# A four-layer graph network on one core: the last layer's messages, products and norm steps in another order

## The chip, the core and the metric

One core of a Trainium2 chip runs the whole program: sixteen independent graphs, one after the other, in 32-bit floats throughout. The engines are named as the profile names them: PE (TensorE, matrix products), PEld (its weight loads), DVE (VectorE), ACT (ScalarE), POOL (GpSimd) and SP (SyncE, which here issues nearly all DMAs). The metric is device microseconds of one execution; lower is better. Before the change three runs took 2419.71, 2419.86 and 2420.47 us, a median of 2419.86 us.

## The reference

For each of 16 graphs there are 1024 nodes with 128 features (`x`) and a 1024 by 1024 weighted adjacency (`adj`). Two networks run in a row, each followed by a residual and a layer norm:

```
# first network
degree = adj.sum(-1)
s      = einsum('bid,bij->bjd', x, adj) / degree
x      = layernorm(x + relu(concat(x, s) @ W.T + b))
# second network: four layers on f (at first f = x)
src_agg = einsum('bjv,bij->biv', f @ ws + bs, adj / l2norm(adj, axis 2))
dst_agg = einsum('bjv,bji->biv', f @ wd + bd, adj / l2norm(adj, axis 1))
f       = tanh(concat(src_agg, f @ wn + bn, dst_agg) @ wu + bu)
# layer three reads f of layers two and one; layer four f of three and two, and x
x       = layernorm(x + f)
```

## The kernel before, in words

**Products.** `wu` is folded into the three other weights ahead of everything, so a layer is: messages (features times folded weights, a DST and a SRC half), then an aggregate (messages times the scaled adjacency and its scaled transpose, added up in PSUM). Each aggregate is a Strassen-Winograd scheme: seven products M1, M2, M3, M4, Z11, Z12, Z21 of half-size operands in place of eight. Its operand sums are made on DVE: `T[2]`, `T[3]`, `T[4]` from the adjacency `a` (for DST), `Q[2..4]` from the transpose `at` (for SRC), and `S[2..4]` from the messages `X` (`message_sums`). The result of M1 to M4 is put together from PSUM by ACT copies and DVE additions into `e0` and `e12`.

**Two columns of PE.** Each product uses 64 of PE's 128 columns, and `aggregate` writes out two lists, `upper` and `lower`, that run side by side. `in_turn` interleaves them. The numbers in `events` and `hooks` are positions in `upper`: at that position the named function's instructions are issued to their engines, ahead of the product of that position.

**Order of work.** The program is scheduled by hand: each engine executes its instructions in the order in which the Python code emits them, and waits on semaphores where data or buffers demand it. In one turn of the loop over `b` the second network of graph `b` runs, with the first network of graph `n = b + 1` and the norm of graph `b - 1` slipped in: layer one (`aggregate` with `l` 0), layer two (`l` 1), layer three's messages (`paired_messages` with `l` 2) and aggregate, then the first network of graph `n` (`first_gnn`), then layer four's messages (`l` 3) and aggregate. Fifteen turns prepare a next graph; the sixteenth doesn't.

**Where the norm of the next graph sits.** Its steps are functions handed to layer four: `add0`, `spread0`, `sum0`, `centre0`, `squares0` by the dictionary `between`, called at the places `at(0)` to `at(4)` of `paired_messages`, and `rstd0`, `rows0`, `end0`, `quarters0`, `rows1`, `rows2` by `hooks` of its aggregate. `centre0` holds a small PE product (`pm`), and an ACT square; `squares0` a DVE reduction to `v`; `rstd0` a small PE product of `v` (`pv`), the DVE sum `ve`, and a power on POOL (line 456); `end0` the DVE multiplication by it (line 461), and `quarters0` the next graph's `T[2]` and `T[3]` (lines 678 and 680).

**Column norms of the next graph.** In layer two of graph `b` the column sums of squares of graph `n` are reduced to `part` (line 344). `inverses` multiplies them on PE (`pc`), takes them to DVE and raises them on POOL (line 376); `inverse_rows`, called by `factors`, finishes them on DVE, writes them to DRAM (`dr`, line 402), and `factor_row` reads them back as a row on all partitions (`cinv`, line 408). The sixteen multiplications of line 414 scale the next adjacency by it.

**Banks.** PSUM has eight banks here: two for Z0 and Z1, four that rotate under the tag `pt` (message products, and `Bk`, `A`, `Dk`, `Ck` for M2, M1, M3, M4), and two that rotate under the tag `small`. M3's SRC part is accumulated in `A` once M1 has been copied out of it.

Of the kernel before, what the change touches and what calls it, by code (L numbers as in the profile page):

```python
# [15 lines left out]
NL = 4  # L16
CHUNKS = [1, 1, 2, 3]
G = 4
# [5 lines left out]
def adj_resnorm_kernel(ctx: ExitStack, tc: tile.TileContext, x, adj, w0, b0, layers, out):  # L24
# [33 lines left out]
    nc = tc.nc  # L58
# [12 lines left out]
    def blocks(ap):  # L71

        return ap.rearrange("p (k g c) -> p g k c", g=G, c=C)
# [627 lines left out]
                between[n]()  # L701
        return message_sums(b, l, t) if with_sums else t

    def message_sums(b, l, t, amid=lambda: None):
# [7 lines left out]
        amid()  # L712
        nc.vector.tensor_sub(S[2], S[1], X[0, 0])
        nc.vector.tensor_sub(S[4], X[0, 1], S[2])
        return X, S
# [9 lines left out]
    def paired_messages(b, l, w, wm, rest=None, between={}):  # L725

        t = [one.tile([P, NJ, 2, 2, V], F32, tag=f"t{j}", name=f"t{l + 1}_{b}_{j}") for j in range(2)]
        X = {(v, j): t[j][:, :, :, v] for v in range(2) for j in range(2)}
        y, s, T2, T4 = w["y"], message_seven(wm), w["T2"], w["T4"]
        T3 = w["e0"] = one.tile([P, HW], F32, tag="e0", name=f"e0_{l}_{b}")  # L730
        o = own_seven(l, wm)
        w["own"] = {"M1": (o["w00"], y[0, 0]), "M2": (o["S2"], T2), "M3": (o["S3"], T3), "M4": (o["S1"], y[0, 1]),
                    "Z11": (o["w01"], y[1, 0]), "Z12": (o["S4"], y[1, 1]), "Z21": (o["w11"], T4)}

        def bank(i):
            return product(f"pt{l + 1}_{b}_{i}")

        def parts(pt):
            return pt.rearrange("p (k a c) -> p k a c", k=NJ, a=2)

        def into(pt, *terms):
            for i, (f, x) in enumerate(terms):
                for k in range(NJ):
                    by_halves(pt[:, k * P:(k + 1) * P], f[:, k * P:(k + 1) * P], x, i == k == 0,
                              i == len(terms) - 1 and k == NJ - 1)
            return pt

        def plain(v, h):
            return [(rest[:, half(h)], wm[:, MREST + v * P:MREST + (v + 1) * P])] if rest is not None else []

        def bias(v):
            return wm[:, v * P:(v + 1) * P].rearrange("p (a c) -> p a c", a=2)[:, None].to_broadcast([P, NJ, 2, V])

        def add(to, x, pt):
            nc.vector.tensor_add(X[to], X[x], parts(pt))  # L755

        def add_sbuf(to, x):
            nc.vector.tensor_add(X[to], X[to], X[x])  # L758

        def add_bias(to, x, v):  # L760
# [12 lines left out]
        if l == 2:  # L773
            m4 = into(bank(4), (y[0, 1], s["S1"]))
            nc.scalar.copy(X[1, 1], parts(m4))
            m1 = into(bank(1), (y[0, 0], s["w00"]))
            add_bias((0, 0), parts(m1), 0)
            at(0)
            t3()
            t4()  # L780
            z12 = into(bank("z12"), (y[1, 1], s["S4"]))
            m2 = into(bank(2), (T2, s["S2"]))
            add((0, 1), (0, 0), m2)
            m3 = into(bank(3), (T3, s["S3"]))
            add((1, 0), (0, 1), m3)
            at(1)
            add_sbuf((0, 1), (1, 1))
            add((0, 1), (0, 1), z12)
            z11 = into(bank("z11"), (y[1, 0], s["w01"]))
            add((0, 0), (0, 0), z11)  # L790
            z21 = into(small(f"pt{l + 1}_{b}_z21", [HW]), (T4, s["w11"]))
            at(2)
            add_bias((1, 0), X[1, 0], 1)
            add_sbuf((1, 1), (1, 0))
            add((1, 0), (1, 0), z21)
        else:
            t4()
            t3()
            m4 = into(bank(4), (y[0, 1], s["S1"]))
            nc.scalar.copy(X[1, 1], parts(m4))  # L800
            at(0)
            m1 = into(bank(1), (y[0, 0], s["w00"]))
            add_bias((0, 0), parts(m1), 0)
            at(1)
            z11 = into(bank("z11"), (y[1, 0], s["w01"]), *plain(0, 0))
            at(2)
            z12 = into(bank("z12"), (y[1, 1], s["S4"]), *plain(0, 1))
            m2 = into(bank(2), (T2, s["S2"]))
            add((0, 1), (0, 0), m2)
            add((0, 0), (0, 0), z11)  # L810
            at(3)
            m3 = into(bank(3), (T3, s["S3"]))
            add((1, 0), (0, 1), m3)
            add_bias((1, 0), X[1, 0], 1)
            add_sbuf((0, 1), (1, 1))
            add((0, 1), (0, 1), z12)
            add_sbuf((1, 1), (1, 0))
            z21 = into(small(f"pt{l + 1}_{b}_z21", [HW]), (T4, s["w11"]), *plain(1, 0))
            add((1, 0), (1, 0), z21)
            p11 = into(bank("p11"), *plain(1, 1))  # L820
            add((1, 1), (1, 1), p11)
        XS = message_sums(b, l, t, lambda: at(4))
        if l == 2:
            at(3)
        return XS

# [27 lines left out]
    def aggregate(b, l, feats, msgs, wm, a, at, T, Q, fT, etag, hooks={}, pieces=1, w=None):  # L854
# [9 lines left out]
        else:  # L864
            e0, e12 = w["e0"], w["e12"]
            Bk, A, Dk, Ck = (product(f"m{i}_{l}_{b}") for i in (2, 1, 3, 4))
        e1, e2 = e12[:, 0], e12[:, 1]
        Z0, Z1 = (product(f"z{h}_{l}_{b}", h) for h in range(NH))

# [22 lines left out]
            nc.scalar.copy(e1[low], e0[high])  # L892

        def m3_read():
            nc.vector.tensor_add(e0[high], e0[high], A[high])
            nc.scalar.copy(e1[high], e0[high])

        def second_half():
# [54 lines left out]
        else:  # L953
            rest = [(f, c) for f, c in feats if c not in PAIRED[l]]

            own_of = {name: [(x, blocks(f))] for name, (x, f) in w["own"].items()}
            m3, m3s = prod("M3", DST), prod("M3", SRC)
            shared = [[(*m3[-1], slice(i * HW // 2, (i + 1) * HW // 2))] for i in range(2)]
# [23 lines left out]
            else:  # L982
                upper = [
                    (Z1, True, own(1, 1, rest)), (Z0, True, own(1, 0, rest)), *own_upper,
                    (A, False, m1), (Bk, False, m2[:NJ]), (A, True, m3s[:1] + shared[1]),
                    (Bk, False, m2[NJ:]), (A, False, m3s[1:]),
                    (Z0, False, prod("Z21", SRC) + prod("Z21", DST)),
                ]
                lower = [
                    (Z1, True, own(0, 1, rest)), (Z0, True, own(0, 0, rest)), *own_lower,  # L990
                    (Dk, False, m3[:2]), (Ck, True, m4[:NJ]), (Dk, False, m3[2:-1]), (Ck, False, m4[NJ:]),
                    (Z1, False, z12[:1]), (Dk, False, shared[0]), (Z1, False, z12[1:]), (Z0, False, prod("Z11", SRC) + prod("Z11", DST)),
                ]
                events = {13: m1_read, 17: m4_read, 19: m3_half, 23: m2_and_half_of_m3, 26: last_reads}

        for i, (o, x, y_, start, stop) in in_turn(flat_steps(upper, high), flat_steps(lower, low)):
            if i in events:
# [235 lines left out]
    for b in range(B):  # L1233
# [162 lines left out]
            p.update(begin_paired(b, 2, f1, f2, "acc"))  # L1396

        hooks = alongside(hooks, {11: y4, 27: t2})
        if b == 0:
            hooks = alongside(hooks, {12: lambda: weight_sums(own_seven(3, None))})  # L1400
        aggregate(b, 1, feats, t, wm, a, at, T, Q, f23, "row", hooks)
        wm = ahead["wm"]
        if b:
            second_norm, xs2 = w, w.get("xs")
            if nxt:
                inverses(n, st)


        feats = [(f1, 1), (f23, 0)]
# [72 lines left out]
        if nxt:  # L1482
# [35 lines left out]
            def place(i, a=a):  # L1518
                return a[:, 2 * i:2 * i + 2].rearrange("p k (u c) -> p (k u) c", c=NH * P)

            def rows0():
                for i, q in enumerate((2, 3)):
                    rows[q] = load_rows(n, q, [place(i)])
                half_of_rows(1, 1, "sq", two)

            def end0(w=w):
                norm_end(w["ys"], w["r"], KS)
                w["x1"] = one.tile([P, N], F32, tag="xb", name=f"x1_{n}_T")
                for h in range(NH):
                    x1_features(n, w["ys"], h, w["x1"])  # L1530
                w["kept"] = put_aside(n, w["ys"])

            def quarters0(w=w):
                half_of_rows(0, 1, "acc")
                w["T"] = combined(n, "T")
                for i in (2, 3):
                    combine(i, y2, w["T"])
                scale_rows(rows[2], 2, rinv)

            def rows1(w=w):  # L1540
# [7 lines left out]
                scale_rows(rows[1], 1, rinv)  # L1548

            between = {0: add0, 1: spread0, 2: sum0, 3: centre0, 4: squares0}  # L1550
            hooks = {7: rstd0, 11: rows0, 14: end0, 18: quarters0, 23: rows1, 27: rows2}
        else:
            x1v = one.tile([P, N], F32, tag="x", name="x1_last")
            for h in range(NH):
# [83 lines left out]
```

## Time and profile before

| what | us |
|---|---|
| median of three runs | 2419.86 |
| the profiled execution's own time | 2422.51 |
| its span, first to last instruction | 2420.7 |
| PE busy | 2391.8 (99%) |
| DVE busy | 2086.4 (86%) |
| ACT busy | 973.3 (40%) |
| POOL busy | 274.4 (11%) |
| POOL power of 128x32, mean of 30 | 6.387 |
| DVE step over 128x512, line 414, mean of 250 | 0.692 |
| matrix product of 512 columns, mean | 0.592 to 0.594 |

A row of the timeline reads: start, length, engine, line, operation, out<-in, shape, count, and in brackets the idle time ahead of it with what ended it. Products overlap in the records: one of 512 columns is shown as 0.59 us long, but in an unbroken stretch one pair, upper and lower, follows the other every 0.429 us, and a 32-bit product is two such passes. A position of `upper` is therefore 0.858 us. A PE that is shown as busy can still be late; the starts have to be compared.

### The profile page before, as it was taken

To read this page: it belongs to the slowest core of one execution; us is meant where nothing else is said; L and a number is where in the kernel's file an instruction comes from. 1 tells how busy PE (TensorE), PEld (TensorE's weight loads), DVE (VectorE), ACT (ScalarE), POOL (GpSimd) and SP (SyncE) were. 2 spreads that over 40 slices of the span, in tenths; PEclk is the share of its full clock that TensorE was granted. 3 is DMA by queue.
4 is the path that set the end of the run, shared out by engine and by line. 5 is a ranking of instruction groups with operands and counts; after the bars stand their busy time and mean duration, and the time that the engine had idled before them with its cause. 6 is when DMAs were issued, how large, how long until landed. Compare 5 with 4: busy or idle time off the path is not lost. (4 is left out here: it accounts for less than half of the span.)

```text
span 2420.7 us, 38913 instructions
## 1 busy us (share of the span) xinstructions
PE 2391.8 (99%) x15293; PEld 1083.8 (45%) x15293; DVE 2086.4 (86%) x2799; ACT 973.3 (40%) x1827; POOL 274.4 (11%) x102
## 2 busy tenths in 40 slices
PE   8999999999999999999999999999999999999998
PEld 4454444444444445444444445444444444444544
DVE  5988989989898998889988899898998989899864
ACT  5524345253342634426244362434525334263322
POOL 4101111011111011110111100111101111101100
PEclk9999999999999999999999999999999999999999
DMA  8627344272533726335282452724427253372400
GB/s 186 139 66 153 69 103 87 71 157 56 127 73 77 149 48 145 71 80 130 48 166 50 97 113 62 154 67 101 90 71 157 57 124 77 78 148 48 99 21 22
DMA packets 365895, 232.01 MB, mean 96 GB/s; under 512 B 152784, under 2 KB 336848, under 8 KB 365712
## 3 DMA queue, kind: packets, MB, share of 16 engines
q1 hardware_dynamic: 364944, 227.16, 43.4%
q0 software_dynamic: 768, 2.36, 0.4%
q8 instruction: 121, 1.98, 0.4%
q14 instruction: 62, 0.51, 0.1%
HBM read 209.59 MB, written 19.84 MB: 95 GB/s over the span
## 5 line engine op out<-in xcount | busy, mean ns | idle before, releaser
L1001 PE MATMUL m<-Q,S 128*64 128x512 f32 x1008 | 450.7, 593 | 0.0
L1001 PE MATMUL m<-at,t 128*64 128x512 f32 x1008 | 439.3, 594 | 0.0
L1001 PE MATMUL m<-T,S 128*64 128x512 f32 (+1 forms) x1072 | 439.2, 567 | 0.0
L1001 PE MATMUL m<-a,t 128*64 128x512 f32 x1008 | 425.1, 593 | 0.0
L456 POOL TENSOR_TENSOR rs<-ve,mhalf 128x32 f32<-128x32 f32 x30 | 191.6, 6387 | 1938.0 <-DVE ve L454 1938.0
L1001 PEld LDWEIGHTS m<-Q,S 128*64 128x64 f32 x1008 | 135.6, 137 | 266.9 <-issue 248.5
L883 ACT COPY e<-m 64x512 f32<-64x512 f32 x63 | 36.6, 582 | 516.1 <-PE m L1001 515.7
L1001 PE MATMUL z<-at,S 128*64 128x512 f32 x504 | 229.2, 592 | 0.0
L1001 PE MATMUL z<-at,t 128*64 128x512 f32 x504 | 229.2, 592 | 0.0
L1001 PE MATMUL z<-a,S 128*64 128x512 f32 x504 | 227.0, 593 | 0.0
L1001 PE MATMUL z<-a,t 128*64 128x512 f32 x504 | 226.8, 592 | 0.0
L1001 PE MATMUL z<-Q,t 128*64 128x512 f32 x504 | 226.6, 592 | 0.1
L1001 PEld LDWEIGHTS m<-T,S 128*64 128x64 f32 x1072 | 134.7, 137 | 150.7 <-issue 137.4
L1001 PEld LDWEIGHTS m<-a,t 128*64 128x64 f32 x1008 | 127.3, 137 | 116.2 <-issue 109.1
L1001 PEld LDWEIGHTS m<-at,t 128*64 128x64 f32 x1008 | 129.2, 137 | 112.0 <-issue 99.4
L1001 PE MATMUL z<-T,t 128*64 128x512 f32 x384 | 172.8, 592 | 0.0
L414 DVE TENSOR_TENSOR a<-a,cinv 128x512 f32<-128x512 f32 x250 | 154.2, 692 | 15.0 <-DMA cinv<-dr 6.8
L322 ACT ACTIVATE sq<-a 128x1024 f32<-128x1024 f32 x120 | 126.0, 1051 | 66.7 <-DVE acc L331 63.3
L1001 PEld LDWEIGHTS z<-Q,t 128*64 128x64 f32 x504 | 69.0, 137 | 142.7 <-issue 141.1
L317 ACT ACTIVATE a<-a 128x1024 f32<-128x1024 f32 x120 | 124.9, 1042 | 0.0
L247 PE MATMUL pt<-wm,f1T 128*64 128x128 f32 (+1 forms) x1536 | 120.6, 310 | 0.0
L331 DVE TENSOR_TENSOR acc<-acc,sq 128x1024 f32<-128x1024 f32 x90 | 110.0, 1222 | 7.2 <-ACT sq L322 3.6
(295 smaller groups left out, 4725.1 us busy)
## 6 DMA issues: line engine op xcount, KB each, us to landing
a<-in_adj_dram SPq DMA_DIRECT2D x120, 512.0 KB, 13.3
rows<-in_adj_dram SPq DMA_DIRECT2D x480, 64.0 KB, 2.1
a<-in_adj_dram SPq DMA_DIRECT2D x240, 128.0 KB, 4.2
wm<-wsave SPq DMA_DIRECT2D x32, 704.0 KB, 5.3
wm<-wsave SPq DMA_DIRECT2D x31, 320.0 KB, 3.8
xn<-in_x_dram SPq DMA_DIRECT2D x124, 64.0 KB, 5.5
xs<-in_x_dram SPq DMA_DIRECT2D x60, 128.0 KB, 3.6
cinv<-dr SPq DMA_DIRECT2D x30, 256.0 KB, 6.4
```

The lines of the kernel that those rows point to most:

```text
L247: nc.tensor.matmul(out[s], x[:, s], y, start=start, stop=stop)
L317: nc.scalar.activation(a[:, i, :], a[:, i, :], AF.Copy, accum_out=degree)
L322: nc.scalar.activation(sq, a[:, i, :], AF.Square, accum_out=state["cols"][:, i:i + 1])
L331: nc.vector.tensor_add(state["acc"], state["acc"], state[i])
L414: engine.tensor_mul(a[:, i, s], a[:, i, s], cinv[:, s])
L456: nc.gpsimd.tensor_tensor(rstd, ve, mhalf[:, :n], ALU.pow)
L883: nc.scalar.copy(e0[high], A[high])
L1001: nc.tensor.matmul(o, x, y_, start=start, stop=stop)
```

## The change

Seven edits, six of them in layer four.

1. Layer four's message products come in the order M4, M1, M2, Z11, M3, Z12, Z21 (before: M4, M1, Z11, Z12, M2, M3, Z21), and the places `at(1)` to `at(4)` move with them. `at(4)` (`squares0`) now stands ahead of `message_sums` instead of in its middle.
2. In its aggregate the order is M1's first half of DST, M2's DST, M3's SRC, then M1's rest; below, M3's DST without a break, then M4.
3. M3's SRC part gets a bank `G` of its own from the tag `small`, in layer four alone. The reads (`events`) move.
4. The hooks: `rstd0` at 5 (before 7); `rows0` is split: the first quarter of rows and the next graph's `T[2]` at 11 (`quarter0`), the other rows at 15 with `end0` (before 14), which also makes the next `T[3]`. `quarters0` at 18 loses both.
5. Layer three: `at(1)` goes from behind M3's addition to ahead of Z12's and M2's products. For `b` of 1 and more that is `factors`; for `b` 0 nothing hangs there.
6. Layer two, for `b` of 1 to 14: `inverses` is issued at hook 29, one position ahead of the aggregate's end, and no longer behind it.
7. `message_sums` loses its argument `amid`.

```diff
         if l == 2:
...
             t4()
+            at(1)
             z12 = into(bank("z12"), (y[1, 1], s["S4"]))
             m2 = into(bank(2), (T2, s["S2"]))
             add((0, 1), (0, 0), m2)
             m3 = into(bank(3), (T3, s["S3"]))
             add((1, 0), (0, 1), m3)
-            at(1)
...
         else:
...
             at(1)
-            z11 = into(bank("z11"), (y[1, 0], s["w01"]), *plain(0, 0))
-            at(2)
-            z12 = into(bank("z12"), (y[1, 1], s["S4"]), *plain(0, 1))
             m2 = into(bank(2), (T2, s["S2"]))
             add((0, 1), (0, 0), m2)
-            add((0, 0), (0, 0), z11)
-            at(3)
+            at(2)
+            z11 = into(bank("z11"), (y[1, 0], s["w01"]), *plain(0, 0))
             m3 = into(bank(3), (T3, s["S3"]))
             add((1, 0), (0, 1), m3)
             add_bias((1, 0), X[1, 0], 1)
+            z12 = into(bank("z12"), (y[1, 1], s["S4"]), *plain(0, 1))
             add_sbuf((0, 1), (1, 1))
+            at(3)
+            add((0, 0), (0, 0), z11)
+            add_sbuf((1, 1), (1, 0))
             add((0, 1), (0, 1), z12)
-            add_sbuf((1, 1), (1, 0))
             z21 = into(small(f"pt{l + 1}_{b}_z21", [HW]), (T4, s["w11"]), *plain(1, 0))
             add((1, 0), (1, 0), z21)
             p11 = into(bank("p11"), *plain(1, 1))
             add((1, 1), (1, 1), p11)
-        XS = message_sums(b, l, t, lambda: at(4))
+            at(4)
+        XS = message_sums(b, l, t)
...
+            if l == NL - 1:
+                G = small(f"m3s_{l}_{b}", [HW])
...
-                    (A, False, m1), (Bk, False, m2[:NJ]), (A, True, m3s[:1] + shared[1]),
-                    (Bk, False, m2[NJ:]), (A, False, m3s[1:]),
+                    (A, False, m1[:2]), (Bk, False, m2[:NJ]), (G, True, m3s[:1] + shared[1]), (A, False, m1[2:]),
+                    (Bk, False, m2[NJ:]), (G, False, m3s[1:]),
...
-                    (Dk, False, m3[:2]), (Ck, True, m4[:NJ]), (Dk, False, m3[2:-1]), (Ck, False, m4[NJ:]),
-                    (Z1, False, z12[:1]), (Dk, False, shared[0]), (Z1, False, z12[1:]), ...
+                    (Dk, False, m3[:-1]), (Ck, True, m4[:NJ]), (Dk, False, shared[0]), (Ck, False, m4[NJ:]),
+                    (Z1, False, z12), ...
-                events = {13: m1_read, 17: m4_read, 19: m3_half, 23: m2_and_half_of_m3, 26: last_reads}
+                events = {14: m3_half, 18: m4_read, 19: m1_read, 23: m2_and_half_of_m3, 26: last_reads}
...
+        if b and nxt:
+            hooks = alongside(hooks, {29: lambda: inverses(n, st)})
...
-            if nxt:
-                inverses(n, st)
...
-            def rows0():
-                for i, q in enumerate((2, 3)):
-                    rows[q] = load_rows(n, q, [place(i)])
+            def quarter0(w=w):
+                w["T"] = combined(n, "T")
+                combine(2, y2, w["T"])
+                rows[2] = load_rows(n, 2, [place(0)])
+
+            def end0(w=w):
+                rows[3] = load_rows(n, 3, [place(1)])
                 half_of_rows(1, 1, "sq", two)
-
-            def end0(w=w):
                 norm_end(w["ys"], w["r"], KS)
                 w["x1"] = one.tile([P, N], F32, tag="xb", name=f"x1_{n}_T")
                 for h in range(NH):
                     x1_features(n, w["ys"], h, w["x1"])
                 w["kept"] = put_aside(n, w["ys"])
+                combine(3, y2, w["T"])
 
             def quarters0(w=w):
                 half_of_rows(0, 1, "acc")
-                w["T"] = combined(n, "T")
-                for i in (2, 3):
-                    combine(i, y2, w["T"])
                 scale_rows(rows[2], 2, rinv)
...
-            hooks = {7: rstd0, 11: rows0, 14: end0, 18: quarters0, 23: rows1, 27: rows2}
+            hooks = {5: rstd0, 11: quarter0, 15: end0, 18: quarters0, 23: rows1, 27: rows2}
```

More of the change, by code (lines that the diff above doesn't have):

```diff
@@ L702, in messages, with message_sums @@
         return message_sums(b, l, t) if with_sums else t
-    def message_sums(b, l, t, amid=lambda: None):
+    def message_sums(b, l, t):
         S = {i: one.tile([P, NJ, 2, V], F32, tag=f"S{i}", name=f"S{i}_{l + 1}_{b}") for i in (2, 3, 4)}
@@ L711, in message_sums @@
         nc.vector.tensor_add(S[1], X[1, 0], X[1, 1])
-        amid()
         nc.vector.tensor_sub(S[2], S[1], X[0, 0])
@@ L866, in aggregate @@
             Bk, A, Dk, Ck = (product(f"m{i}_{l}_{b}") for i in (2, 1, 3, 4))
+        G = A
         e1, e2 = e12[:, 0], e12[:, 1]
@@ L894, in m3_read @@
         def m3_read():
-            nc.vector.tensor_add(e0[high], e0[high], A[high])
+            nc.vector.tensor_add(e0[high], e0[high], G[high])
             nc.scalar.copy(e1[high], e0[high])
@@ L990, in aggregate @@
                     (Z1, True, own(0, 1, rest)), (Z0, True, own(0, 0, rest)), *own_lower,
-                    (Dk, False, m3[:2]), (Ck, True, m4[:NJ]), (Dk, False, m3[2:-1]), (Ck, False, m4[NJ:]),
-                    (Z1, False, z12[:1]), (Dk, False, shared[0]), (Z1, False, z12[1:]), (Z0, False, prod("Z11", SRC) + prod("Z11", DST)),
+                    (Dk, False, m3[:-1]), (Ck, True, m4[:NJ]), (Dk, False, shared[0]), (Ck, False, m4[NJ:]),
+                    (Z1, False, z12), (Z0, False, prod("Z11", SRC) + prod("Z11", DST)),
                 ]
-                events = {13: m1_read, 17: m4_read, 19: m3_half, 23: m2_and_half_of_m3, 26: last_reads}
+                events = {14: m3_half, 18: m4_read, 19: m1_read, 23: m2_and_half_of_m3, 26: last_reads}
         for i, (o, x, y_, start, stop) in in_turn(flat_steps(upper, high), flat_steps(lower, low)):
```

## The prediction, made before the changed kernel was run

> **What bounds the kernel now.** I read the page first: PE is busy for 2391.8 of 2420.7 us. So only three things can help: less PE work, and there is none less here (same products, same sizes), or fewer moments at which PE is late. The waits of PE name three of interest (us in total, times, longest):
>
> ```profile
> PE pw L247 <- DVE e_f L577: 2.7, 5, 0.8
> PE pw L247 <- DVE e_f L585: 2.7, 10, 0.3
> PE pv L252 <- DVE v L446: 2.6, 14, 0.2
> ```
>
> That counts only time in which no product is in flight, so it understates. I therefore cut the turn that prepares graph 12 into its stages and compared each with its product pairs at 0.4292 us (windows: stretch, length, then busy time and count of PE, PEld, DVE, ACT, POOL):
>
> ```profile
> 1793.88:1797.64 3.76, 3.65 (x19) 1.08 (x17) 3.59 (x6) 0.69 (x1) 0.00 (x0) 1.00 0.00 0
> 1807.36:1836.64 29.28, 29.10 (x145) 9.91 (x143) 22.70 (x27) 11.00 (x25) 7.39 (x2) 1.00 0.73 144
> 1840.09:1866.58 26.49, 26.49 (x123) 12.07 (x120) 24.88 (x27) 13.26 (x26) 0.00 (x0) 1.00 0.82 170
> 1870.07:1896.14 26.07, 26.07 (x134) 9.02 (x132) 23.89 (x28) 17.00 (x31) 5.43 (x1) 1.00 0.23 49
> ```
>
> First row, `pw` of the first network (its last eight pairs, which need DVE's `e_f`): 8 pairs are 3.43, a turn without wait takes 3.49, this one is 0.27 over that. Second, layer four's aggregate: 67 pairs are 28.76, and `pv` itself 0.14; 0.39 is lost. Third, the next graph's layer one: 60 pairs are 25.75; 0.74 is lost, though PE is shown busy all the time. Fourth, layer two: 25.75 and three small products of 0.11: nothing lost. All turns are alike but for `pw`, whose fourteen lengths (graphs 2 to 15) run from 3.49 to 5.02 and sum to 57.2, 8.3 over 14 x 3.49; one first network is also 0.33 late.
>
> Each loss has its cause in the timeline. Layer four: PE waits for `v`, and DVE, later, 5.32 us for POOL's power, which makes everything behind it late:
>
> ```profile
> 1812.46 1.21 DVE L446 TENSOR_REDUCE v<-sq 128x32 f32<-128x1024 f32 x1
> 1813.59 0.68 DVE L713 TENSOR_TENSOR S<-t 128x512 f32<-128x512 f32 x1
> 1814.30 0.69 DVE L714 TENSOR_TENSOR S<-t,S 128x512 f32<-128x512 f32 x1
> 1814.91 0.18 DVE L454 TENSOR_SCALAR ve<-pv 128x32 f32<-128x32 f32 x1
> ...
> 1822.61 1.23 DVE L461 TENSOR_TENSOR y<-y,rs 128x1024 f32<-128x1024 f32 x1 [5.32 <-POOL inv L309]
> ...
> 1838.69 0.65 DVE L1003 TENSOR_TENSOR e<-e,z 128x512 f32<-128x512 f32 x1
> ```
>
> Line 1003 runs 2.05 us after PE ended this aggregate (1836.64); DVE never catches up in layer one. There its S[3] ends at 1842.19, so the lower column starts at 1842.34 and not 1841.81; its Q[2] ends at 1856.18, and PE starts on it 0.05 later:
>
> ```profile
> 1842.34 0.61 PE L1001 MATMUL m<-T,S 128*64 128x512 f32 x1
> ...
> 1856.23 0.64 PE L1001 MATMUL m<-Q,S 128*64 128x512 f32 x1
> ```
>
> `pw`: DVE waits for the row `cinv`, and from there to `pw` DVE has no slack:
>
> ```profile
> 1753.77 0.16 DVE L397 TENSOR_TENSOR cols<-cols,inv 128x8 f32<-128x8 f32 x1
> ...
> 1762.96 1.29 DVE L414 TENSOR_TENSOR a<-a,cinv 128x512 f32<-128x512 f32 x2 [0.32 <-DMA cinv<-dr]
> ```
>
> In graphs 2 to 15 this wait runs from 0.05 to 1.93, turn by turn about 0.05 above the lateness of `pw`, and sums to 8.9.
>
> **What the skill says.** The Trainium skill, "TensorE: Matmul & The Clock Gate", Part 3 (The mechanism): products start and end in program order. The trace agrees: at 1813.72 both columns stand still for `pv`. "SBUF — State Buffer" (Who interferes with whom): a DVE step with two SBUF inputs and a GpSimd step that reads SBUF exclude each other. It fits: the power takes 7.34 us here, where line 682 (two inputs, 1815.01 to 1817.29) began just before it, and 5.43 in layer two, where POOL began first. "PSUM — Partial Sum Buffer" (The four PSUM rules): a product that opens a sum discards what the bank's partitions held, so M3 in `A` had to wait for M1's copies. No lateness shows there, so I give the bank `G` nothing.
>
> **Layer four's messages.** The DVE steps are the same, in another order; independent ones of 512 follow each other every 0.60, dependent ones every 0.725, the ones of 1024 add 1.13 to 1.2. From 1799.93, the end of `add0`: bias 1800.53, transpose 1801.68, M2 1802.28, sum `s` 1803.42, M3 1804.02, bias 1804.75, add 1805.35, centring 1806.48 (before 1806.51), five additions 1809.50, reduction `v` 1810.64 (before 1813.67), S[3] 1811.30, S[1] 1812.04, S[2] 1812.76, S[4] 1813.49, `ve` 1813.6 (before 1815.09). PE's messages cost the same 9.72. A product over 512 nodes takes 0.874; `pm` now stands behind eight of them (Z11 and Z12 count twice), at 1797.64 + 8 x 0.874 = 1804.6, and its sum is there at 1803.4; ACT does the square in 1806.5 to 1807.6, ahead of the reduction.
>
> PE reaches position 5 at 1807.36 + 10 x 0.429 = 1811.65, 1.0 after `v`. S[3] is wanted at 1811.79 and M2's S[2] at 1813.5; a weight load needs S 0.15 earlier, so 0.3 to 0.6 remain. **Gain 14 x 0.39 = 5.4.** Graph 1 has no `pv` wait but 0.50 before `pm`; `pm` comes 0.87 later, its sum 0.6 later: 0.25.
>
> **Layer four's tail and layer one.** POOL starts at 1813.7, again behind line 682, and ends at 1821.1. The next T[2] fills DVE's gap: PE leaves the old T[2] after 22 units (a unit is one pair, half a position), at 1807.50 + 22 x 0.429 = 1816.9, so 1817.2 to 1819.5. Multiplication and transposes end 1823.7, T[3] 1825.9. Then ACT sets the pace: M4's copies from 1822.7, eight row scalings to 1827.1, and only then M1's copy, to 1827.7. Line 891 starts 1827.7 (before 1829.78), and with the same steps behind it line 1003 starts 1836.6, PE having ended at 1836.25: 0.4 behind and not 2.05. Four additions of line 698 then follow PE, which allows a lag of 1.3. As in layer two, S[3] starts 0.95 after the aggregate's start, in time; from there to the end of Q[2] DVE needs 14.41 (1841.77 to 1856.18), so 15.36 against the wanted 36 x 0.429 - 0.05 = 15.40. That margin is nil, and I leave 0.05 a turn. **Gain 15 x 0.74 - 0.6 = 10.5.** If the tail stays late, nothing.
>
> The row loads: SP issues eight DMAs at hook 11 from about 1816.3 (rows 0 and 1 of `a` are read by M4 up to unit 20), 3.8 us; the 16 that go to hook 15 may start when PE passes unit 29, 1819.9, so SP's queue keeps its pace, and nothing is pushed past another queue. Scaling needs rows 2 at 1823.8; they land 2 us after issue. If they were later, 0.9 us of slack stands between that and layer one.
>
> **Layer three and two.** `pc` at hook 29 goes to PE 0.86 sooner. DVE's three small steps (0.6) fall into a wait of 0.50 for Z0. POOL then runs 1748.9 to 1751.8 (2.90); `factors` stand behind T3 and T4 at 1752.4 and not 1753.77, ahead of M2's and M3's additions, whose readers come after 1757. Write `dr`, two reads `cinv`, then the loads of x and the stores keep their order on SP and all come 1.45 sooner, where the DMA share is 0.01. Waits of 0.05 to 1.06 vanish, 1.93 leaves 0.5. **Gain 8.6 - 0.5 = 8.1.** The price: PE wants `pc` at 1747.61 and `part` is done at 1747.58, seen 0.05 later; a late small product costs 0.05 beyond its wait: 0.08 in thirteen turns, 0.24 in one, **loss 1.3** (bounds 0.4 and 2.8, from half of it and twice).
>
> Sum: 5.4 + 0.25 + 10.5 + 8.1 - 1.3 = 23.0. On the span: 2397.7; the profiled execution is 1.8 above its span and 2.65 above the median, so the median goes from 2419.86 to **2396.9**. All losses together are 5.4 + 0.5 + 11.2 + 8.6 = 25.7: the floor is 2394.
>
> **Rivals.**
> - *The tail stays late* (12%): ACT's scaling of the rows, which stands before M1's copy, waits for DMAs in the busiest DMA stretch (0.73 share). Then layer one keeps its 0.74. For: PE's new order frees the rows 0.5 later; against: 1.5 us of slack. 2407.
> - *`cinv` lands when it did* (12%): the path is DMA latency, 6.6 us, that a sooner start may meet differently; or POOL is late and DVE waits at `factors` instead. Against: in 14 turns it lands 6.6 to 7.2 after issue, with no other traffic. 2405.
> - *Only the wait for `v` goes* (7%): both fail, and some of it comes back at `pc`. 2415.
> - *Slower* (5%): the reduction now stands ahead of S[3] and S[2]; if DVE's real spacing puts them late, PE stops at positions 5 to 8 in every turn. It decides from 0.34 us of slack + 23.0/15 = 1.9 us of lateness on; at 2.5 us, 2429.
>
> The likeliest case (64%) has its own range, 2394 to 2402. Eight in ten reach to the two single failures: 2394 to 2409. A difference under 0.2%, 4.8 us, can hardly be told from none. Faster 0.92, same 0.03, slower 0.05.
>
> **What would show it.** Right: layer four's aggregate at 28.9, layer one's near 25.8, `pw` at 3.5 in every turn, no `cinv` wait on line 414, `pc` late by less than 0.1. Wrong: PE starting late on `m<-T,S` in layer four, line 461 still idle for POOL past 1822, or a DVE wait at line 397.

## The result and the profile after

The changed kernel runs in 2401.33 us (median of five runs, 2400.39 to 2402.42) where the kernel before took 2419.71 us on the same chip (five runs). The ratio is 0.9924, with a 95% interval of 0.991 to 0.9939: faster by 18.4 us, or 0.76%. The forecast of 2396.9 us had the sign and the range right and was 4.4 us too low. The profiled execution took 2401.80 us with a span of 2400.0 us.

PE is still busy 99% of the span. So the same cut into stages is what tells. First PE's waits after the change (waiting step, what it waited for, then us in total, times, longest):

```profile
PE pt L247 <- DMA wm<-wsave: 1.7, 2, 1.2
...
PE pw L247 <- DVE e_f L577: 0.8, 1, 0.8
PE pw L247 <- DVE e_f L585: 0.6, 3, 0.3
```

The wait for `v` is gone, that of `pw` has shrunk from 5.4 to 1.4 us, and there is a new one: layer two's messages (`pt`) wait for their weights `wm`. The four stages of a typical turn, the one that prepares graph 10 (windows: stretch, length, busy time and count of PE, PEld, DVE, ACT, POOL):

```profile
1483.87:1487.41 3.54, 3.54 (x19) 1.88 (x17) 3.37 (x6) 0.57 (x1) 0.00 (x0) 1.00 0.00 0
1497.13:1526.00 28.87, 28.87 (x145) 15.47 (x143) 22.67 (x26) 12.48 (x28) 7.39 (x2) 1.00 0.70 141
1529.46:1555.29 25.83, 25.83 (x124) 11.53 (x122) 24.06 (x26) 11.73 (x23) 0.00 (x0) 1.00 0.91 195
1558.78:1585.03 26.25, 26.25 (x134) 9.06 (x132) 24.36 (x31) 16.99 (x31) 5.43 (x1) 1.00 0.23 48
```

`pw` takes 3.54 (before 3.76 in the turn shown, 3.99 in the median turn), layer four's aggregate 28.87 (29.28), layer one's 25.83 (26.49), and layer two, in which `pc` now stands one position ahead of the end, 26.25 (26.07). Added up over the fifteen turns of each profile, by the starts of PE's products:

| stage, sum of 15 turns | before | after | gain | forecast |
|---|---|---|---|---|
| layer four, messages | 146.40 | 145.97 | 0.4 | 0.25 |
| layer four, aggregate | 438.78 | 433.54 | 5.2 | 5.4 |
| layer one, aggregate | 397.45 | 389.72 | 7.7 | 10.5 |
| first network and `pw` | 244.11 | 237.37 | 6.7 | 8.1 |
| layer two's aggregate and layer three's messages (14 turns) | 450.99 | 453.26 | -2.3 | -1.3 |
| all | | | 17.9 | 23.0 |

Layer three's aggregate and the other messages didn't move. The two spans differ by 2.8 us more than this, because the start-up of the profiled execution before, up to the first of these products, happened to be 2.8 us longer. The comparison of medians, 18.4, agrees with the table.

Layer four's tail goes as forecast. DVE's timeline of the same turn (start, length, engine, line, operation, out<-in, shape, count, and the idle time ahead of it with what ended it):

```profile
1499.13 1.22 DVE L446 TENSOR_REDUCE v<-sq 128x32 f32<-128x1024 f32 x1
...
1503.11 0.18 DVE L454 TENSOR_SCALAR ve<-pv 128x32 f32<-128x32 f32 x1
...
1506.89 2.29 DVE L678 TENSOR_TENSOR T<-a 128x2048 f32<-128x2048 f32 x1 [1.39 <-PE m L1004]
1510.81 1.23 DVE L461 TENSOR_TENSOR y<-y,rs 128x1024 f32<-128x1024 f32 x1 [1.64 <-POOL inv L309]
...
1517.70 0.69 DVE L892 TENSOR_TENSOR e<-e,m 64x512 f32<-64x512 f32 x1 [2.15 <-ACT e L884]
...
1526.61 0.65 DVE L1006 TENSOR_TENSOR e<-e,z 128x512 f32<-128x512 f32 x1
```

The wait of 5.32 us for POOL has become 1.39 for PE and 1.64 for POOL, and behind T[3] there are 2.15 us in which DVE waits for ACT. Line 1006 (1003 before) starts 0.61 after PE's end of the aggregate, and not 2.05.

### The profile page after: what moved, and what is told of

Its sections match the earlier page's. It is cut to its first block, busy times and chain, and to the rows that moved or that the text cites. A ratio compares the mean times of both kernels' runs of the same rounds, so it can differ in the third digit from the quotient of the medians.

```text
span 2400.0 us, 38990 instructions
## 1 busy us (share of the span) xinstructions
PE 2379.0 (99%) x15293; PEld 1299.1 (54%) x15293; DVE 2084.5 (87%) x2799; ACT 974.1 (41%) x1827; POOL 274.3 (11%) x102
## 4 chain that ended last, share of the span: by engine, by line
PE 89%; DMA 5%; DVE 3%; SPq 1%; ACT 1%; issue 1%; POOLq 0%; DVEq 0%; ACTq 0%
PE m L1004 40%; PE z L1004 23%; PE pt L247 9%; PE pt_z L247 5%; PE m_f L583 4%; PE z_f L583 3%; PE m3s L1004 2%; PE pw L247 2%; DMA wm<-wsave 2%; DMA a<-in_adj_dram 1%; SPq L640 1%; PE pt_p L247 1%; PE z L851 1%; DMA wm<-in_L_gnn_ws_dram 1%; DVE a L414 0%
## 5 line engine op out<-in xcount | busy, mean ns | idle before, releaser
L1004 PE MATMUL m<-a,t 128*64 128x512 f32 x1008 | 453.9, 593 | 0.0
L1004 PE MATMUL m<-T,S 128*64 128x512 f32 (+1 forms) x1040 | 429.9, 574 | 0.0
L1004 PE MATMUL m<-at,t 128*64 128x512 f32 x1008 | 423.2, 593 | 0.0
L1004 PE MATMUL m<-Q,S 128*64 128x512 f32 x880 | 393.0, 593 | 0.0
L1004 PEld LDWEIGHTS m<-Q,S 128*64 128x64 f32 x880 | 118.1, 137 | 188.1 <-issue 157.1
L1004 PEld LDWEIGHTS m<-a,t 128*64 128x64 f32 x1008 | 135.8, 137 | 108.0 <-issue 95.5
L884 ACT COPY e<-m 64x512 f32<-64x512 f32 x63 | 36.6, 582 | 323.8 <-PE m L1004 323.1
L906 ACT COPY e<-m 64x512 f32<-64x512 f32 x63 | 36.4, 578 | 219.2 <-PE m L1004 218.4
## 6 DMA issues: line engine op xcount, KB each, us to landing
a<-in_adj_dram SPq DMA_DIRECT2D x120, 512.0 KB, 13.7
```

Source lines behind the costliest of these rows:

```text
L884: nc.scalar.copy(e0[high], A[high])
L906: nc.scalar.copy(e1[high], Dk[low])
L1004: nc.tensor.matmul(o, x, y_, start=start, stop=stop)
```

## The experiments

The theory after the result: layer four's message order starts POOL's power sooner, and both the wait for `v` and layer one's lateness come from that; `cinv` comes sooner; and the missing 5 us went into `pc`, into columns of PE that no longer run in step, and into the weights `wm`. The main rival: the edits' gains are independent of each other, as the forecast's sum had it, and bank `G` and the next `T` beside the norm carry the part of layer one. Every run is timed against the kernel before on the same chip; ratios have 95% intervals.

**Layer four alone.** The changed kernel with edits 5 and 6 undone. What is left are edits 1 to 4 and 7, five of the seven (the section on the change counts six for layer four):

```diff
             t4()
-            at(1)
...
             add((1, 0), (0, 1), m3)
+            at(1)
...
-        if b and nxt:
-            hooks = alongside(hooks, {29: lambda: inverses(n, st)})
...
             second_norm, xs2 = w, w.get("xs")
+            if nxt:
+                inverses(n, st)
```

> Layer four's edits alone (1 to 4 and 7), layers two and three as before. Theory of separate causes: the three losses add up, so layer four's aggregate is 28.87, the next layer one's 25.8, while line 414 waits for cinv again and pw is 4.0 in the median; 5.2 + 0.4 + 7.7 = 13.3 us less than before, about 2406.4. Rival: a DVE that is earlier in layer four is still earlier two layers on, so pw shrinks as well and nearly the whole gain is here, 2401 to 2402.

Measured: 2405.77 us, ratio 0.9949 (0.9934 to 0.9964). Layer four's aggregate is 28.87 and layer one's 25.76 in the typical turn; `pw` is back at a median of 3.87 and layer two at 26.07. By the medians some 12 of the 18 us belong to layer four's edits, as expected. The profiled execution, 2402.15 us, is the fastest of its four (the others took 2405.63 to 2406.59); its stages gain 17.0, of which layer one has 10.2.

**Layers two and three alone.** Edits 5 and 6 on the kernel before (the counterpart of the diff above).

> Edits 5 and 6 alone: the column sums' product one position ahead of layer two's end and factors ahead of M2's product in layer three. Theory: pw 3.54 in most turns, 6.4 us less, and layer two's aggregate 26.25 and not 26.07, 2.1 us more, together some 4.5 us less, about 2415; layer four's aggregate stays at 29.28 and layer one's at 26.49. Rival: the reads of cinv land no sooner relative to DVE, or the late small product eats it all: 2419 to 2422.

Measured: 2415.77 us, ratio 0.9993 (0.9984 to 1.0001). The interval includes 1, so the times alone show no gain (the medians differ by 2.0 us); by the stages of the profile it is 3.9 us. `pw` falls from a sum of 57.2 to 50.8 in 14 turns (50.7 in the changed kernel), and layer two rises from 365.0 to 367.5. Layer four's aggregate loses 0.8 in all, though nothing in it is changed: the first sign that something is handed on from stage to stage. Whether the gains of the two parts add up is not settled: by the medians they come to 14.0 us and the changed kernel has 18.4, by the stages to 20.9 and it has 17.9.

**The reduction to `v` ahead of the sums, alone.** If the wait of PE for `v` is a loss of its own, this should bring its part of the gain. On the kernel before:

```diff
         nc.vector.tensor_add(S[1], X[1, 0], X[1, 1])
-        amid()
...
-        XS = message_sums(b, l, t, lambda: at(4))
+            at(4)
+        XS = message_sums(b, l, t)
```

> Before, with one move: squares0 ahead of message_sums. Theory: v is done about 1.5 us sooner, so PE doesn't wait at pv (aggregate 28.87), 5.2 us; but ve stands behind the same DVE steps, so the power on POOL starts when it did, line 461 still idles 5.3 us for it and layer one stays at 26.49: about 2414.5. Rival: v alone holds the tail, layer one falls to 25.8 too, about 2407.

Measured: 2419.74 us, ratio 1.001 (1.0001 to 1.0018). The expectation failed: the wait for `v` is gone from PE's waits, and not one microsecond is gained. From the start of layer four's aggregate to the end of layer one's a turn takes 59.34 us, before 59.22. The timeline shows why; first DVE, then a product of PE's lower column:

```profile
1505.26 0.69 DVE L754 TENSOR_TENSOR t<-t,pt 128x512 f32<-128x512 f32 x1 [1.03 <-PE pt L247]
...
1512.36 1.21 DVE L446 TENSOR_REDUCE v<-sq 128x32 f32<-128x1024 f32 x1
1513.48 0.75 DVE L710 TENSOR_TENSOR S<-t 128x256 f32<-128x256 f32 x2
...
1516.33 0.18 DVE L454 TENSOR_SCALAR ve<-pv 128x32 f32<-128x32 f32 x1
...
1524.03 1.23 DVE L461 TENSOR_TENSOR y<-y,rs 128x1024 f32<-128x1024 f32 x1 [5.32 <-POOL inv L309]
```

```profile
1513.95 0.64 PE L1001 MATMUL m<-T,S 128*64 128x512 f32 x1
```

The aggregate starts at 1508.66, so `ve` comes 7.67 after it, and before it came 7.55 after (1814.91 - 1807.36). `v` is ready sooner, but `ve` stands behind the message sums on DVE and can't use it. The power, its reader and the whole tail are as late as ever. And PE's wait for `v` is exchanged for another: S[3] now stands behind the reduction, and the first product with it, `m<-T,S`, starts 5.29 after the aggregate's start, where it started 4.30 after it before, a lateness of 1.0 in 14 of the 15 turns. So this run doesn't show what the wait for `v` alone is worth; it shows that DVE has no room there for both. The first line shows where DVE's chain loses time: M2's product stands behind Z11's and Z12's, and DVE waits 1.03 us for it. The kernel before has the same wait once a turn (DVE's waits: total, times, longest, the first one in the head of the kernel being the longest):

```profile
DVE t L755 <- PE pt L247: 17.9, 16, 2.9
```

**The messages' order alone.** Edit 1 with `rstd0` at 5, on the kernel before: the aggregate's order, the banks, the row loads and the next T[2] and T[3] stay as they were.

```diff
             at(1)
-            z11 = into(bank("z11"), (y[1, 0], s["w01"]), *plain(0, 0))
-            at(2)
-            z12 = into(bank("z12"), (y[1, 1], s["S4"]), *plain(0, 1))
             m2 = into(bank(2), (T2, s["S2"]))
             add((0, 1), (0, 0), m2)
-            add((0, 0), (0, 0), z11)
-            at(3)
+            at(2)
+            z11 = into(bank("z11"), (y[1, 0], s["w01"]), *plain(0, 0))
...
-            hooks = {7: rstd0, 11: rows0, 14: end0, 18: quarters0, 23: rows1, 27: rows2}
+            hooks = {5: rstd0, 11: rows0, 14: end0, 18: quarters0, 23: rows1, 27: rows2}
```

> Before, with edit 1 (order of the message products, squares0 ahead of message_sums) and rstd0 at 5; the aggregate's order, the banks, the row loads and the next T[2] and T[3] at 18 stay as before. Theory that the earlier start of POOL's power is what frees the tail: POOL ends 1.5 us sooner, T[2] and T[3] still follow, line 1003 runs about 1.0 us after PE's end, under the 1.3 that layer one bears; layer one 25.8 to 25.9, about 13 us less, 2407. Rival, that T[2] and T[3] in DVE's gap are what frees the tail: layer one stays near 26.4, 5 to 6 us less, 2414.

Measured: 2403.50 us, ratio 0.9944 (0.9927 to 0.9961), like layer_four. Layer four's aggregate takes 28.87 and layer one's 25.76, and the two with the messages between them 58.08. DVE's timeline, with the aggregate starting at 1497.41:

```profile
1491.66 0.65 DVE L754 TENSOR_TENSOR t<-t,pt 128x512 f32<-128x512 f32 x1
...
1503.37 0.18 DVE L454 TENSOR_SCALAR ve<-pv 128x32 f32<-128x32 f32 x1
...
1527.15 0.65 DVE L1003 TENSOR_TENSOR e<-e,z 128x512 f32<-128x512 f32 x1
```

M2's addition no longer waits, `ve` comes 5.96 after the start, 1.6 sooner than before (1.03 of that is the wait that is gone), S[3] is in time though it stands behind the reduction here too, and DVE still waits 5.32 us for POOL. Yet line 1003 runs only 0.87 behind PE's end (1526.28), inside the 1.3 that layer one bears. So edit 1 with `rstd0` at 5, which starts POOL's power 1.6 us sooner, brings the whole gain of layers four and one as far as these runs can tell. Filling DVE's gap with the next `T` brings line 1006 another 0.26 forward (0.61 behind), where nothing waits for it. Bank `G` and the aggregate's new order show no gain either.

**The product of the column sums back behind layer two.** The changed kernel with edit 6 undone, `factors` still ahead of the additions.

> The changed kernel with edit 6 undone: the column sums' product behind layer two's aggregate again, factors still ahead of M2's product in layer three. Theory: layer two falls back to 26.07 (2.3 us less), but DVE now stands 0.6 us for POOL's power at line 397 in each turn, pw is about 3.9 and not 3.54 (5 us more): some 3 us slower than the changed kernel, 2404. Rival: DVE's wait is covered, and only the late product's price goes: 2399.

Measured: 2406.63 us, ratio 0.9955 (0.994 to 0.997), by the ratios some 7 us slower than with edit 6, and 4.9 by the profiled spans. The sign was as expected, and so were the wait at line 397 and `pw`, 3.88 in the median turn; that layer three's own aggregate gets longer, 27.45 and not 27.16, was not foreseen. The group of line 397, the first step of `factors` (busy, mean ns, then idle time and its cause):

```profile
L397 DVE TENSOR_TENSOR cols<-cols,inv 128x8 f32<-128x8 f32 x15 | 2.5, 168 | 7.9 <-POOL inv L376 7.9
```

With the power started late, DVE waits 7.9 us in fifteen turns where it waited for nothing before, and the loss begins at layer three's own sums: S[3] is begun 4.59 us into the aggregate and not 3.96. The aggregate, the first network and `pw` take 43.34 us together in a turn, and 42.72 in the changed kernel. Edit 5 needs edit 6; without it the time (0.9955) is within the interval of layer_four's (0.9949), which has neither. Edit 6 without edit 5 wasn't run.

**`factors` between M2's and M3's additions.** Edit 6 undone as above, and `factors` 0.6 us later against the aggregate, where POOL is done:

```diff
             t4()
-            at(1)
...
             add((0, 1), (0, 0), m2)
+            at(1)
             m3 = into(bank(3), (T3, s["S3"]))
```

> The changed kernel with edit 6 undone and factors between M2's and M3's additions in layer three, where POOL's power is just done. Theory: layer two 26.07, dr 0.8 us sooner than before the change, so waits for cinv of less than 0.8 vanish and the longer ones lose 0.8; pw 3.5 to 3.9; 1 to 2 us less than the changed kernel, about 2400. Rival: the 1.45 us are needed in most turns, pw near 3.8 throughout: 2402 to 2404.

Measured: 2399.30 us, ratio 0.9927 (0.9911 to 0.9944), not to be told from the changed kernel's 0.9924. A typical turn takes 146.15 us, and 146.45 in the changed kernel; `pw` takes 3.43 and layer one 25.78. In return four turns have a late `cinv`, the worst with `pw` at 4.55.

This pair also shows where PE's columns fall out of step. In the changed kernel, layer three (its aggregate starts at 1444.69):

```profile
1448.65 0.76 DVE L710 TENSOR_TENSOR S<-t 128x256 f32<-128x256 f32 x2
1448.99 0.59 PE L1004 MATMUL m<-a,t 128*64 128x512 f32 x1
...
1449.13 0.64 PE L1004 MATMUL m<-T,S 128*64 128x512 f32 x1
1449.41 0.59 PE L1004 MATMUL m<-a,t 128*64 128x512 f32 x1
...
1449.61 0.59 PE L1004 MATMUL m<-T,S 128*64 128x512 f32 x1
```

The same place with `factors` between the additions (aggregate from 1441.97):

```profile
1445.77 0.76 DVE L710 TENSOR_TENSOR S<-t 128x256 f32<-128x256 f32 x2
...
1446.24 0.13 PEld L1004 LDWEIGHTS m<-T,S 128*64 128x64 f32 x1 [0.27 <-DVE S L710]
1446.26 0.59 PE L1004 MATMUL m<-a,t 128*64 128x512 f32 x1
1446.27 0.62 PE L1004 MATMUL m<-T,S 128*64 128x512 f32 x1
```

S[3] is begun 3.96 us into the aggregate in the first and 3.80 in the second; before the change it was 3.77. In the second the lower column's `m<-T,S` starts with its neighbour. In the first it starts 0.14 behind it and the next one 0.20, and so the two columns go on, 0.19 apart by the finer records, through the rest of layer three and the first network; `pw` and the stages behind it pay for it. Before the change the three small steps of `factors` filled the pause between M3's addition and the next step that depends on it; ahead of the additions they fill nothing, and from line 766 (767 before) to S[3] DVE takes 6.88 and not 6.71.

**The column sums and their product sooner still.** The changed kernel, with `column_sums` at hook 21 instead of 24 and `inverses` at 27 instead of 29:

```diff
-                                ... 20: sums_of(of=(6,)), 21: sums_of(add=(7,)),
-                                23: sums_of(of=(7,)), 24: lambda: column_sums(n, st)}
+                                ... 20: sums_of(of=(6,)), 21: last_sums,
+                                23: sums_of(of=(7,))}
...
-            hooks = alongside(hooks, {29: lambda: inverses(n, st)})
+            hooks = alongside(hooks, {27: lambda: inverses(n, st)})
```

(`last_sums` is `add_squares(n, st, 7)` and `column_sums(n, st)`.)

> The changed kernel with the column sums (lines 339 and 344) moved from hook 24 to hook 21 of layer two, ahead of the last reads, and inverses from hook 29 to 27, ahead of layer three's first T2. Theory: part is done some 2 us sooner, so PE doesn't wait at pc; layer two's aggregate 26.1 and not 26.25, pw as before or lower, 2 us less than the changed kernel, 2399. Rival: the last reads come 2.4 us later, the tanh of layer two's second half too, and PE waits for T2 in layer three's messages: layer three's messages over 6.3 us, 2401 to 2405.

Measured: 2397.28 us, ratio 0.9918 (0.9903 to 0.9932), by which it can't be told from the changed kernel's 0.9924; the profile shows more. `part` is done 0.4 ahead of `pc`, layer two takes 26.10, and a turn 146.28. `pw` stays at 3.51 and layer one at 25.84: with `pc` in time the columns still run 0.17 apart from layer three on. So that part of the loss isn't `pc`'s; it is `factors`'.

**Layer two's weights between the halves of the load.** The changed kernel loads `wm` behind the whole next adjacency. Here the second half of that load is issued behind `wm`:

```diff
-                w["a"] = load(n)
+                w["a"] = load(n, (0,))
...
                 ahead["wm"] = message_weights(b, 1)
+                if nxt:
+                    load(n, (1,), w["a"])
```

> The changed kernel with layer two's weights loaded ahead of the second half of the next adjacency. Theory: in the changed kernel they land behind the whole adjacency, 2.3 us ahead of layer two's messages in most turns and too late in two or three (0.73, 1.35 and 0.13 us of waiting); now they land 8 us ahead and these waits go, 1 to 2 us less, 2400. Rival: the adjacency's second half then lands too late for ACT's squares, part is late and pc waits longer: 2402 to 2406.

Measured: 2399.87 us, ratio 0.9926 (0.9911 to 0.9941). The wait for `wm` is gone and layer one's sum falls from 363.9 to 362.4 in 14 turns. That is about what the profile shows of the wait, and too little for the ratio to tell. The tile `wm` in the turn of graph 14, in the changed kernel (issue, and time to landing):

```profile
L238 SPq DMA_DIRECT2D wm<-wsave x1: 345/345/345, 2122.7 to 2122.7; - x1
...
DMA to landing us min/median/max: 20.0/20.0/20.0
```

and with the halves split:

```profile
L238 SPq DMA_DIRECT2D wm<-wsave x1: 345/345/345, 2117.8 to 2117.8; - x1
...
DMA to landing us min/median/max: 12.2/12.2/12.2
```

The Trainium skill, "DMA: Bandwidth & Descriptors", Issuing engines are not separate DMA queues, says that DMAs end up on the same 16 DMA engines and interleave, whichever engine started them. Loads and weights come from one queue here, SP's, so no run tests that for several; the trace shows them sharing: the weights take 20.0 us behind eight loads of 512 KB and 12.2 behind four. In the changed kernel they land at 2142.7, and PE has waited 1.2 us for them.

**Combinations, and the changed kernel beside them.** All four ran on one chip. The first is sums_sooner with weights_first:

> The changed kernel with two repairs together: the column sums at hook 21 and their product at hook 27 (as in sums_sooner), and layer two's weights between the halves of the adjacency's load (as in weights_first). Theory: the three late spots of the changed kernel are the product of the column sums (2.2 us in all), the weights that land late in two or three turns (0.7, 1.4, 0.1), and write-read round trips that take twice as long in two turns (0.5 each). The repairs concern different stages, so they add up: sums_sooner ran at 0.9918 and weights_first at 0.9926 of the time before, the changed kernel at 0.9924; expected 0.9912 to 0.9916, about 2396. Every turn 146.3, no wait for wm, none for pc. Rival: nothing is left to gain because the pace of the product pairs is the limit and the rest is spread; then 0.992, 2398 to 2400.

Measured: 2397.27 us, ratio 0.9916 (0.9902 to 0.993). The second is factors_between with weights_first:

> The changed kernel with the product of the column sums back behind layer two, factors between M2's and M3's additions (as in factors_between), and layer two's weights between the halves of the load. Theory: no small product is late, so the two columns stay together and the typical turn is 146.15; what is left over are single turns in which the row cinv lands late because it is requested 1.4 us later than in the other repair (two of about one us in factors_between). Expected: pw 3.43 typical with up to three outliers, layer one 25.78 without a wm wait, ratio 0.9912 to 0.992, 2395 to 2398. Rival: the outliers come in more turns, and it loses to sums_and_weights by 2 us or more.

Measured: 2397.55 us, ratio 0.9918 (0.9904 to 0.9931). The third puts the messages' order, `factors` between the additions and the split load on the kernel before, and leaves out bank `G`, the aggregate's order, the next `T` beside the norm and hook 29:

> The kernel before with three small edits: layer four's message products in the new order (as in messages_alone, old aggregate order, no bank G, T[2] and T[3] at hook 18), factors between M2's and M3's additions in layer three, and layer two's weights between the halves of the load. Theory: bank G, the aggregate's new order and the next T[2] and T[3] beside the norm bring nothing by themselves, so this small edit is as fast as between_and_weights: ratio 0.9912 to 0.992, layer four's aggregate 28.87, layer one 25.78. Rival: the new aggregate gives DVE the slack that keeps single turns from being late; then this one is slower than between_and_weights by 2 us or more, with the lateness in layer one.

Measured: 2396.53 us, ratio 0.9913 (0.99 to 0.9927). The changed kernel itself on that chip:

> The changed kernel itself, on the chip of the three combinations, to compare with them directly. Expected 0.9924 of the time before, as measured already (0.991 to 0.9939); all three combinations 2 to 3 us below it, if the theory of its three late spots holds, and equal to it if not.

Measured: 2399.30 us, ratio 0.9926 (0.9913 to 0.994). So the combinations are 1.8 to 2.8 us below the changed kernel, at the lower edge of what was expected; the split load shows in the traces and hardly in the times (sums_sooner alone had 0.9918). The smallest edit is at least as fast as any. Its runs, 2394.91 to 2398.26, all lie below those of the changed kernel, 2398.98 to 2401.38; the difference of 2.8 us is 0.12%, and between the three combinations nothing can be told. Its `pw` and layer one in one turn (columns as above):

```profile
1481.69:1485.12 3.43, 3.43 (x18) 1.30 (x16) 3.26 (x6) 0.62 (x1) 0.00 (x0) 1.00 0.00 0
...
1527.16:1552.93 25.77, 25.77 (x122) 9.57 (x120) 23.99 (x26) 11.95 (x24) 0.00 (x0) 1.00 0.86 181
```

Both are at the pace of their product pairs, as are layer four at 28.87 and layer two at 26.07. A turn takes 146.13 us, and what is lost beside that is in single turns, most of them with a late `cinv`: `pw` is 3.55 to 4.39 in five of the 14 turns behind the first.

## Why the prediction was right, and where its sizes were off

**Layer four's messages** (forecast 5.4 and 0.25; measured 5.2 and 0.4). The size is right. Fourteen turns gain 0.41 each, `v` ends 3.22 after the aggregate's start (forecast 3.28) and `ve` starts 5.98 after it (6.24). Graph 1's aggregate lost 0.44: there `v` ends 4.34 after the start, `pv` is 0.19 late, and PE's weights wait 0.74 for S[2], which stands behind the reduction. The cause as given, PE's wait for `v`, is only half of it: squares_first removed that wait and gained nothing, since S[3] then came late. It is the sooner start of the whole chain on DVE that makes room for both.

**The tail and layer one** (forecast 10.5; measured 7.7). Each time from the aggregate's start came within 0.3 us:

| step | forecast | measured |
|---|---|---|
| POOL's power ends | 13.7 | 13.65 |
| next T[2] starts | 9.8 | 9.76 |
| T[3] ends | 18.5 | 18.42 |
| first line behind M1's copy starts | 20.3 | 20.57 |
| line 1003, now 1006 | 29.2 | 29.48 |

So the mechanism holds, but the step that put the gain down to T[2] in DVE's gap and to ACT as the pace gave the credit to the wrong edit: messages_alone has layer one at 25.76 with the gap left open. The sum bore this out only because the kernel has both edits. The mis-sized term is the 0.6 of losses (0.05 in 15 turns is 0.75 in any case); it was 3.3 over 25.76 a turn. Two turns waited for `wm`, 0.73 and 1.43 over it. The forecast named what was pushed past a queue in layer four and overlooked that a shorter layer one brings its end nearer to a DMA that doesn't move: `wm` landed 2 to 4 us before its use in the kernel before, and 1 to 3 in the changed one where it came in time. In two turns Q[2] was late, and layer one took 0.18 and 0.27 longer, where the forecast had called the margin nil; in a third, 0.20 longer, layer two's messages had to wait for their features `f1T`. Columns out of step cost 0.07 in seven others; where `pw` had waited long (3.72, 4.02, 4.03) they were in step again, and layer one took 25.76.

**`cinv` and `pw`** (forecast 8.1; measured 6.7). No turn but graph 1's lies above 4.03, and 11 of the 14 that the forecast counted stand at 3.54 to 3.56. Its sum of what is left over was 0.5 and measured 1.85: 0.55 from 11 turns 0.05 over 3.49, 0.5 each from two turns, 0.2 from one. The 0.05 comes from the step that let `factors` go "ahead of M2's and M3's additions, whose readers come after 1757": S[3], whose first step starts 5.7 us behind the first of them (1442.94 to 1448.65 in the changed kernel), has no slack at all. The two turns are the write `dr`: it took 2.94 and 2.69 us there, and 1.42 to 1.46 in nine of fifteen. The Trainium skill, "DMA: Bandwidth & Descriptors", Latency and other measured facts, gives 0.2 us for an HBM access on average and 2 us at high load. A spread of 1.5 us fits that size, but not its cause: DMA share was 0.06 in the write of 2.94 and 0.08 in one of 1.43. It isn't chance alone: in five profiles, those of the changed kernel (on two chips), sums_sooner, weights_first and sums_and_weights, the writes above 2 us are the same six, for graphs 1, 2, 7, 9, 11 and 13. What makes them slow stays open; the best version still has slow ones.

**`pc` at hook 29** (forecast -1.3, bounds -0.4 and -2.8; measured -2.3). The price per turn was 0.05 seen late and 0.05 for a late small product. The reduction ends, then the weight load runs, then the product (timeline of one turn):

```profile
556.70 1.22 DVE L344 TENSOR_REDUCE part<-acct 128x32 f32<-128x1024 f32 x1
...
558.03 0.23 PEld L252 LDWEIGHTS pc<-part,fold 128*64 128x64 f32 x4 [0.81 <-issue]
558.06 0.31 PE L252 MATMUL pc<-part,fold 128*64 128x32 f32 x4
```

`part` ends at 557.92 and `pc` starts 0.14 later; PE had wanted it at 557.94. So PE gets `part` 0.14 after its end and not 0.05, and `pc` is 0.12 late and not 0.02 to 0.03. Layer two pays 0.18 in all turns but one, of which layer three's messages give back 0.03, where the forecast had 0.08 in all. This term of the sum was mis-sized; the sign of the whole edit was right, since product_later is slower without it.

**Rivals.** None came as a whole. The tail isn't late, `cinv` lands sooner, and S[3] and S[2] of layer four are in time but for graph 1, where what the rival *Slower* described did happen. The nearest to what happened elsewhere was the remark that POOL may be late and DVE wait at `factors`; it took the removal of edit 6 to see that.

**What would show it.** Layer four 28.9: yes. Layer one near 25.8: yes in the typical turn. `pw` 3.5 in every turn: in all but three. No `cinv` wait on line 414: two turns, 0.19 and 0.40. `pc` late by less than 0.1: no, 0.12.

## What to carry to other kernels

Look for the first late step of a chain and not for the engine's last wait: here the losses of layer four's messages and aggregate and of the next layer one went when DVE's chain came 1.6 us sooner, 1.03 of it a wait for one product near its head; moving one step ahead to end the last wait only made the next step late. A step that is moved to fill an engine sooner also leaves the place where it had filled a pause; count from there to the next step that has no slack. And when a stage gets shorter, look at every transfer that it used to cover, moved or not.

## What the runs showed of the hardware that was not expected

A lateness of 0.14 us in one of PE's two columns did not heal by itself: in the changed kernel the columns stay 0.19 us apart for 37 us, over layer three and the first network, then 0.09 for another 58, though the trace shows no wait of one for the other, and are back in step (0.01) only at layer one's Q[2], for which PE waits. A DMA write of 16 KB took 1.42 to 1.46 us in nine turns and 2.17 to 2.94 in the others, 3.52 in one of the other kernels. In four of these turns, two with a short write and two with a long one, the DMA share during the write was 0.06 to 0.08, so no traffic in the trace explains the difference, and the long ones came in the same turns in five profiles.
